# Self-attention of a two-layer decoder: four heads stored side by side at each key

## The chip, the core and the metric

The kernel runs on one NeuronCore of a Trainium2 chip. It computes in five engines: TensorE (PE; its weight loads are shown on a line of their own, PEld), VectorE (DVE), ScalarE (ACT), GpSimd (POOL) and SyncE (SP), which here only issues DMAs. The metric is the time of one execution on the device in microseconds (us), as a median over runs. All data is 32-bit floating point unless said otherwise, so one element is 4 bytes.

## The reference, cut to what matters

Eight batches of 256 tokens with 256 features go through two layers. Layer 0 is a gated recurrence, a cross-attention and a small feed-forward with quantised weights. Layer 1 is a self-attention with relative positions, a cross-attention and a gated feed-forward. Each step ends in a residual sum and a layer norm. The change touches layer 1's self-attention, with 16 heads of 16 features:

```python
idx = jnp.clip(pos[None, :] - pos[:, None], -MAX_REL, MAX_REL) + MAX_REL   # MAX_REL = 20
rk2, rv2 = rel_k[idx], rel_v[idx]
attn1 = jnp.einsum('bhqd,bhkd->bhqk', q, k)
attn2 = jnp.einsum('bhqd,qkd->bhqk', q, rk2)
attn = jax.nn.softmax((attn1 + attn2) / scale, axis=-1)
w1 = jnp.einsum('bhqk,bhkd->bhqd', attn, v)
w2 = jnp.einsum('bhqk,qkd->bhqd', attn, rv2)
```

Only 41 distances count: outside the band of 20 keys to either side of the query, all distances look alike.

## The kernel before, in words

**The order of the work.** Nothing is left to a scheduler at run time. While the program is built, the class `Order` (L87) plays the whole kernel through with costs that are written beside each step, and writes out the instructions of each engine in the order that this gives. A step asks for an engine, a cost in us, the times at which its inputs are ready, and buffers (`Slots`, `Held`). A DMA is given bytes and a rate in GB/s (`dma`, L208); the planner lets transfers follow one another on one memory clock (`memory`, L191). Each engine then runs its list in that order on the chip and waits where an input is late.

**Three attentions with one body.** The items of layer 0's cross-attention (`item_x0`, ai = 0), layer 1's self-attention (`item_s1`, ai = 1) and layer 1's cross-attention (`item_x1`, ai = 2), eight of each, share the functions `quad`, `head`, `values`, `scales` and `attend_out`. A quad is four heads, `head_of(n, j)` for j from 0 to 3, all even or all odd heads of one half c of the features. For each quad:

- PE computes scores into four PSUM banks, one per head, 2 x 256 wide (L914).
- DVE adds a bias to the scores, and finds the row minimum of the negated sum (L942; 256 keys an instruction). In cross-attention the bias is a mask tile; in self-attention it is the band of the quad, `band[:, j]`.
- ACT takes the exponential into `p[:, j, q, :]` and sums the row (L958; 256 keys an instruction).
- PE transposes `p[:, j]` in four pieces of 128 x 128 (L503, where `p` is the operand that is loaded as weights), and ACT or DVE copies the PSUM bank to a `pts` buffer (L291, L292). There are eight `pts` buffers. The buffer is asked for after the transposition (L976).
- PE multiplies by the values (L998).

In all three attentions `p` is [128, 4 heads, 2, 256 keys]: the 256 keys of one head lie next to one another.

**What self-attention does besides.** `to_scratch` (L1306) multiplies the queries with the 41 distances for all eight heads of a half (`drel`, L1317), copies the product to `w`, [128, 8 heads, 104], has POOL spread the last distance over the rest of each row (L1327), and writes it to a scratch array in HBM, `sk`. `to_bands` (L1346) reads `sk` back along diagonals, so that a distance becomes a key: four DMAs for each quad, which write the band tiles, [128, 4 heads, 2, 256 keys]. After the exponentials, `tails_task` (L1386) writes the part of `p` that lies in the band to a second scratch array, `pb` (L1399), and sums the rest: POOL cuts it out of `p` (L1410, L1415), DVE reduces it (L1426). The diagonals of `pb` come back as sums for each distance into `acc`, [128, 2, 2, 8 heads, 41] (L1434), `acc` is transposed (L1468) and multiplied with the relative values (L1483). The sums of the exponentials are kept in `acc` too, and `scales` takes their reciprocal (L1022).

Every one of these DMAs moves runs as long as the innermost stretch that is contiguous on both sides: 104 keys or fewer of one head for `sk`, `band` and `pb` (416 or 336 bytes), 39 distances of one head for `acc` (156 bytes).

**What overlaps.** The self-attention items and the cross-attention items of layer 1 are interleaved by `S1_AT` and `X1_AT` (L785). Band tiles are used from 309 to 653 us of the span.

Of the kernel before, what the change touches and what calls it, by code (L numbers as in the profile page):

```python
# [86 lines left out]
class Order:  # L87
# [51 lines left out]
    def run(self):  # L139
        while self.tasks:  # L140
# [3 lines left out]
            for task in sorted(self.tasks, key=lambda t: (t[0] >= FILLER, t[0], t[1])):  # L144
# [3 lines left out]
                if needs:  # L148
                    slots = needs[0].slots
                    if id(slots) in kept:  # L150
                        continue
                    if len(slots.idle) < len(needs):
                        if ready <= self.clock + 0.5:
                            kept.add(id(slots))
                        continue
                    slots.idle.sort()
                    ready = max(ready, slots.idle[len(needs) - 1][0])
# [17 lines left out]
            if best is None:  # L175
                ahead = [t[3][3] for t in self.tasks if t[3][0] == "get" and t[3][3] > self.clock + 0.5]
                if not ahead:
                    raise RuntimeError(f"stuck: {[t[3][:2] for t in self.tasks]}")
                self.clock = min(ahead)
                continue  # L180
            for held in task[3][4]:
                held.take(*held.slots.idle.pop(0))
# [40 lines left out]
def kernel(  # L223
# [119 lines left out]
    drel = const.tile([P, HH, NR], F32, name="drel")  # L343
# [5 lines left out]
    zero = w0.tile([P, LPAD], F32, name="zero")  # L349
    nc.gpsimd.memset(zero, 0.0)  # L350
    sk, pb = {}, {}
    for pr in range(2):
        for t in range(NQ):
            for c in range(KC):
                sk[pr, t, c] = scratch.tile(
                    [HH, P, SKW], F32, tag=f"sk{pr}{t}{c}", name=f"sk{pr}{t}{c}"
                )
        pb[pr] = scratch.tile([KC, NQ, HH, P, PBW], F32, tag=f"pb{pr}", name=f"pb{pr}")
# [71 lines left out]
    def loads_rel():  # L430
# [9 lines left out]
        for (pr, q, c), d in sk.items():  # L440
# [3 lines left out]
                    out=d[:, :, 0:LPAD].rearrange("h p w -> p h w"),  # L444
                    in_=zero.unsqueeze(1).to_broadcast([P, HH, LPAD]),
                ),
                90,
            )
        for d in pb.values():
            for c in range(KC):  # L450
                for q, (z0, p0) in enumerate(((0, 0), (PBW - MR, P - BLK))):
# [3 lines left out]
                            out=d[c, q, :, p0 : p0 + BLK, z0 : z0 + MR].rearrange("h p w -> p h w"),  # L455
                            in_=zero[p0 : p0 + BLK, 0:MR].unsqueeze(1).to_broadcast([BLK, HH, MR]),
# [3 lines left out]
        def tables():  # L460
            nc.vector.tensor_tensor(
                drel, blocks, blocks[:, :, 0:1].to_broadcast([P, HH, NR]), ALU.subtract
            )
# [8 lines left out]
        events["rel"] = yield from do("DVE", 0.8, [t], tables)  # L472
# [325 lines left out]

    def project_q(it, srcT, t_src):
# [153 lines left out]
    def head(it, n, j, p, s, nm, t, left, times):  # L953
        h = head_of(n, j)

        def emit():
            for q in range(NQ):
                nc.scalar.activation(  # L958
                    p.tile[:, j, q, :], s.tile[:, q, :], AF.Exp, bias=nm[:, q : q + 1], scale=-1.0,
# [12 lines left out]
        t = yield from do("PE", TURNS, [t_e, ps], lambda: transposed(ps.tile, p.tile[:, j]))  # L972
# [3 lines left out]
        pts = yield from get(pts_bufs, f"pts{it.name}_{n}_{j}", t)  # L976
# [41 lines left out]
    def scales(it):  # L1018
# [3 lines left out]
        t = yield from do("DVE", 0.3, [t_s], lambda: nc.vector.reciprocal(  # L1022
            rs.rearrange("p t (c h) -> p t c h", c=KC), it.sums_all()
        ))
# [102 lines left out]
    def item_x0(b):  # L1127
        it = Item(0, b, b, "l0a", "l0x")
        it.sum_of = lambda t, h: it.sums[:, t, h : h + 1]
        it.sums_all = lambda: it.sums.rearrange("p t (c h) -> p t c h", c=KC)  # L1130
# [135 lines left out]
    def layer1_self():  # L1266
        rel = layer1s.enter_context(tc.tile_pool(name="rel", bufs=1))
        kr_bufs = slots(rel, "kr", 2, [P, KC, 2, S - BW])
        wide_bufs = slots(rel, "wide", 2, [P, HH, PBW])
        acc_bufs = slots(rel, "acc", 2, [P, KC, NQ, HH, NA])  # L1270
# [4 lines left out]
        for n in range(3):  # L1275
            bands.append(rel.tile([P, 4, NQ, S], F32, name=f"band{n}"))
# [8 lines left out]
    def cleared(bands):  # L1285
        def emit():
            flat = t.rearrange("p j t k -> p (j t k)").rearrange("p (n k) -> p n k", k=P)
# [7 lines left out]
    def item_s1(b, kr_bufs, wide_bufs, acc_bufs, tail_bufs, at_bufs, band_bufs):  # L1295
# [7 lines left out]
        it.sum_of = lambda t, h: it.acc.tile[:, h // HH, t, h % HH, 0:1]  # L1303
        it.sums_all = lambda: it.acc.tile[:, :, :, :, 0].rearrange("p c t h -> p t c h")

        def to_scratch(c, t_sk):  # L1306
            q = it.q.tile
            out = []
            ends = it.ends[c] = small.tile([P, NQ, HH], F32, tag="ends", name=f"ends{b}_{c}")
            t_e = 0.0  # L1310
            for t in range(NQ):
# [6 lines left out]
                        flat(), q[:, c, t * P : (t + 1) * P], drel.rearrange("p h r -> p (h r)"),  # L1318
# [3 lines left out]
                rows_ = flat().rearrange("p (h r) -> p h r", r=NR)  # L1322
                t_w = yield from copy([t_p, w.at], w.tile[:, :, 0:NR], rows_, HH * NR)
                ps.drop(t_w)

                def emit():
                    nc.gpsimd.tensor_copy(  # L1327
                        w.tile[:, :, NR:], w.tile[:, :, NR - 1 : NR].to_broadcast([P, HH, PBW - NR])
                    )
                    nc.gpsimd.tensor_copy(ends[:, t, :], w.tile[:, :, NR - 1])  # L1330
# [6 lines left out]
                        out=sk[b % 2, t, c][:, :, LPAD:].rearrange("h p w -> p h w"), in_=w.tile  # L1337
                    ),
                    180,
# [6 lines left out]
        def to_bands(c, times, sk_set):  # L1346
            for i in range(2):
# [4 lines left out]
                def emit():  # L1352
                    for t, lo, hi in ((0, BLK + MR, BW), (1, P + BLK + MR, S)):
                        nc.gpsimd.tensor_copy(  # L1354
                            band.tile[0:BLK, :, t, lo:hi],
                            it.ends[c][0:BLK, t, i:HH:2].unsqueeze(2).to_broadcast([BLK, 4, hi - lo]),
# [4 lines left out]
                for t in range(NQ):  # L1361
                    for g in range(P // BLK):
# [4 lines left out]
                                out=band.tile[g * BLK : (g + 1) * BLK, :, t, lo:hi],  # L1367
                                in_=diagonals(
                                    sk[b % 2, t, c], 4, 2 * P * SKW, SKW - 1,
                                    i * P * SKW + g * BLK * SKW + LPAD + lo - k0, hi - lo,  # L1370
                                ),
                            ),
                            180,
# [12 lines left out]
        def tails_task(n, p, left, t_p):  # L1386

            c = n // 2
            own = slice(n % 2, HH, 2)
# [475 lines left out]
```

## Time and profile before

| what | before |
|---|---|
| median of 3 runs | 821.1 us (819.34 to 821.84) |
| profiled execution: span from first to last instruction | 807.4 us |
| what lies around the span, against the median | 13.7 us |
| mean granted TensorE clock | 0.998 |
| busy PE / DVE / ACT / POOL | 774.9 / 703.4 / 629.7 / 210.4 us |
| DMA packets on SP's queue | 177574, of which all but some 22500 are under 512 bytes |
| share of the 16 DMA engines' time that these packets take | 43.4% |

The profiled execution is given by its span alone; its own time is not listed apart from the three runs, so that what lies around the span is taken as 821.1 - 807.4 = 13.7 us, and a change of the span as a change of the time.

A group of instructions is shown as: line, engine, operation, written tile <- read tiles, shapes, count, then busy us and mean ns of one, then the idle time of the engine just before them with what ended it. Consecutive instructions of an engine overlap, so that a pace (start to start) is read from the timeline and not from the mean of one.

### The profile page before, as it was taken

The page shows a single profiled execution, that of the slowest core. Times are in us where ns is not written, and L with a number is a line of the kernel's source. Part 1 is how long each engine was busy: PE and PEld are TensorE (multiplying, and loading weights), DVE is VectorE, ACT ScalarE, POOL GpSimd, SP SyncE. Part 2 cuts the span into 40 slices and gives each one's busy share as a digit, 9 for nine tenths or more (in the row PEclk, how much of TensorE's full clock was granted, in tenths as well). Part 3 has the DMA queues.
Part 4 walks back from the last instruction along what each step waited for, and adds up shares of the span by engine and source line. Part 5 has one row for each costly group of instructions (what it writes and reads, how often), then busy time and mean ns, then how long its engine had stood idle before and what let it go on. Part 6 is the DMA issues. An engine that isn't in the chain of part 4 may idle for free. (4 is left out here: it accounts for less than half of the span.)

```text
span 807.4 us, 21273 instructions
## 1 busy us (share of the span) xinstructions
PE 774.9 (96%) x7175; PEld 597.3 (74%) x7175; DVE 703.4 (87%) x2461; ACT 629.7 (78%) x2036; POOL 210.4 (26%) x398
## 2 busy tenths in 40 slices
PE   7999999999999999997999999999999999999995
PEld 6787777777766787665767677767776767899885
DVE  3998989989787698887799999898898999989986
ACT  2339999899988457786597799999999899845942
POOL 4440321122111044233333304313242323110010
PEclk9999999999999999999999999999999999999999
DMA  5736352100100449889978706743656333100001
GB/s 183 221 120 97 26 74 50 40 15 28 40 14 15 144 116 220 173 166 154 192 159 170 137 7 145 166 87 89 121 120 139 85 72 114 40 15 16 26 14 39
DMA packets 177681, 77.67 MB, mean 96 GB/s; under 512 B 155046, under 2 KB 171430, under 8 KB 177574
## 3 DMA queue, kind: packets, MB, share of 16 engines
q1 hardware_dynamic: 177574, 76.32, 43.4%
q8 instruction: 57, 0.93, 0.5%
q14 instruction: 50, 0.41, 0.2%
HBM read 41.66 MB, written 34.64 MB: 94 GB/s over the span
## 5 line engine op out<-in xcount | busy, mean ns | idle before, releaser
L958 ACT ACTIVATE p<-sn,nm 128x256 f32<-128x256 f32 x768 | 381.5, 510 | 14.1 <-DVE nm L942 8.2
L503 PE MATMUL pt<-ident,p 128*128 128x128 f32 x1536 | 208.4, 278 | 4.3 <-ACT p L958 1.8
L503 PEld LDWEIGHTS pt<-ident,p 128*128 128x128 f32 x1536 | 169.4, 141 | 50.5 <-ACT p L958 30.2
L292 ACT COPY pts<-pt 128x512 f32<-128x512 f32 x277 | 148.3, 591 | 34.5 <-PE pt L503 29.6
L958 ACT ACTIVATION_READ_ACCUMULATOR p<-sn,nm 128x1 f32 x768 | 154.4, 201 | 0.0
L914 PE MATMUL s<-k,q 32*128 32x256 f32 (+2 forms) x1792 | 118.6, 370 | 0.5 <-ACT pts L292 0.3
L998 PE MATMUL pv<-pts,v 128*32 128x256 f32 x1536 | 104.0, 385 | 0.0
L942 DVE CUSTOM_DVE_ANT_0 sn<-s,bias 128x256 f32<-128x256 f32 x256 | 93.1, 419 | 10.0 <-ACT p L958 5.8
L942 DVE CUSTOM_DVE_ANT_0 sn<-s,hide 128x256 f32<-128x256 f32 x256 | 92.8, 418 | 8.2 <-PE s L914 5.3
L942 DVE CUSTOM_DVE_ANT_0 sn<-s,band 128x256 f32<-128x256 f32 x256 | 92.3, 418 | 8.6 <-PE s L914 3.5
L914 PEld LDWEIGHTS s<-k,q 32*128 32x128 f32 x1792 | 77.2, 185 | 30.1 <-issue 20.1
L291 DVE COPY pts<-pt 128x512 f32<-128x512 f32 x107 | 71.1, 683 | 6.7 <-PE pt L503 6.3
L998 PEld LDWEIGHTS pv<-pts,v 128*32 128x32 f32 x1536 | 41.7, 109 | 41.5 <-issue 19.1
L942 DVE DVE_READ_ACCUMULATOR2_ANT nm<- 128x1 f32 x768 | 63.0, 82 | 0.0
L1028 POOL COPY rsw<-rsum 128x512 f32<-128x512 f32 x24 | 14.6, 610 | 157.4 <-DVE rsum L1022 139.0
L520 PE MATMUL pso<-wvo,oT 128*128 128x256 f32 x192 | 46.3, 385 | 0.4 <-ACT pts L292 0.4
L520 PEld LDWEIGHTS pso<-wvo,oT 128*128 128x128 f32 x192 | 35.1, 190 | 7.8 <-issue 1.3
L1354 POOL COPY band<-ends 64x256 f32<-64x256 f32 x64 | 21.5, 360 | 70.8 <-DVE nm L942 70.8
L1426 DVE TENSOR_REDUCE acc<-tail 128x8 f32<-128x864 f32 x32 | 33.4, 1045 | 5.3 <-POOL tail L1415 5.3
L1327 POOL COPY w<-w 128x504 f32<-128x504 f32 x32 | 19.6, 613 | 68.8 <-DVE w L291 40.7
L1709 ACT ACTIVATE sg<-fg 128x512 f32<-128x512 f32 x24 | 14.3, 599 | 21.7 <-PE fg L1698 21.6
L520 PE MATMUL psv<-wvo,ctxT 128*128 128x256 f32 x128 | 30.8, 384 | 0.0
(197 smaller groups left out, 1321.3 us busy)
## 6 DMA issues: line engine op xcount, KB each, us to landing
sk<-w SPq DMA_DIRECT2D x32, 416.0 KB
band<-sk SPq DMA_DIRECT2D x64, 104.0 KB
pb<-p SPq DMA_DIRECT2D x64, 104.0 KB
band<-sk SPq DMA_DIRECT2D x64, 84.0 KB
pb<-p SPq DMA_DIRECT2D x64, 84.0 KB
acc<-pb SPq DMA_DIRECT2D x32, 156.0 KB
ctxT<-in_ctxT SPq DMA_DIRECT2D x16, 256.0 KB
wpad<-in_qk_w SPq DMA_DIRECT2D x6, 512.0 KB
```

Of the source, the lines that this page charges most:

```text
L291: ("DVE", on_dve(n), lambda: nc.vector.tensor_copy(dst, src)),
L292: ("ACT", on_act(n), lambda: nc.scalar.copy(dst, src)),
L503: nc.tensor.transpose(ps[:, c, t * P : (t + 1) * P], src[:, t, c * P : (c + 1) * P], ident)
L520: nc.tensor.matmul(ps[:, t, :], srcT[:, c, t * P : (t + 1) * P], w[:, c, :], start=(c == 0), stop=(c == KC - 1),)
L914: nc.tensor.matmul(ps[j].tile[:, t, first : first + w], it.q.tile[32 * j : 32 * j + 32, c, t * P : (t + 1) * P], k[32 * j : 32 * j + 32, c ...
L942: nc.vector.tensor_tensor_reduce(out=s.tile[:, t, :], in0=ps[j].tile[:, t, :], in1=tile[:, t, :], scale=-1.0, scalar=3e38, op0=ALU.add, op ...
L958: nc.scalar.activation(p.tile[:, j, q, :], s.tile[:, q, :], AF.Exp, bias=nm[:, q : q + 1], scale=-1.0, accum_out=it.sum_of(q, h),)
L998: nc.tensor.matmul(it.pv.tile[32 * j : 32 * j + 32, c, :], it.v.tile[:, k, head_of(n, j), :], pts.tile[:, k, :], start=(k == 0 and i == 0 ...
L1028: lambda: nc.gpsimd.tensor_copy(wide.tile.rearrange("p t (h d) -> p t h d", d=DH), rs.unsqueeze(3).to_broadcast([P, NQ, H, DH]),),
L1327: nc.gpsimd.tensor_copy(w.tile[:, :, NR:], w.tile[:, :, NR - 1 : NR].to_broadcast([P, HH, PBW - NR]))
L1354: nc.gpsimd.tensor_copy(band.tile[0:BLK, :, t, lo:hi], it.ends[c][0:BLK, t, i:HH:2].unsqueeze(2).to_broadcast([BLK, 4, hi - lo]),)
L1426: lambda: nc.vector.tensor_reduce(acc[:, c, :, own, 1], tail.tile, AX.X, ALU.add),
```

## The change

Wherever self-attention keeps four heads of a quad, the head becomes the innermost index. `drel` and `w` become [.., 2, 41 or 104, 4], `sk` and `pb` [.., row, key, 4], the bands [128, 2, 256 keys, 4], `acc` [.., 2, 41, 4]. Self-attention's `p` keeps its buffer but is read through `beside` and `probs` as [128, 2, 256 keys, 4]; the two cross-attentions use `p` as before. A run of a DMA is then four times as long (1664, 1344 or 624 bytes), the number of DMAs is the same, and an engine that works on one head of a band, of `p` or of `acc` finds its elements 16 bytes apart.

```diff
+    def beside(p):
+        return p.rearrange("p j t k -> p (j t k)").rearrange("p (t k j) -> p t k j", t=NQ, j=4)
+    def probs(it, p):
+        return p if it.whole else beside(p).rearrange("p t k j -> p j t k")
...
-                    p.tile[:, j, q, :], s.tile[:, q, :], AF.Exp, bias=nm[:, q : q + 1], scale=-1.0,
+                    probs(it, p.tile)[:, j, q, :], s.tile[:, q, :], AF.Exp, bias=nm[:, q : q + 1], scale=-1.0,
...
-        t = yield from do("PE", TURNS, [t_e, ps], lambda: transposed(ps.tile, p.tile[:, j]))
+        pts = Held(pts_bufs, f"pts{it.name}_{n}_{j}")
+        t = yield from do("PE", TURNS, [t_e, ps, pts], lambda: transposed(ps.tile, probs(it, p.tile)[:, j]))
...
-        pts = yield from get(pts_bufs, f"pts{it.name}_{n}_{j}", t)
...
-            bands.append(rel.tile([P, 4, NQ, S], F32, name=f"band{n}"))
+            bands.append(rel.tile([P, NQ, S, 4], F32, name=f"band{n}"))
...
-            quad(it, 0, parts, lambda n, j: (it.bands[n].tile[:, j], 0.0)),
+            quad(it, 0, parts, lambda n, j: (it.bands[n].tile[:, :, :, j], 0.0)),
...
-                                out=band.tile[g * BLK : (g + 1) * BLK, :, t, lo:hi],
+                                out=band.tile[g * BLK : (g + 1) * BLK, t, lo:hi, :].rearrange(
+                                    "p k j -> p (k j)"
+                                ),
...
-                            180,
+                            280,
...
-                            in_=p.tile[rows_, :, t, lo:hi],
+                            in_=beside(p.tile)[rows_, t, lo:hi, :].rearrange("p w j -> p (w j)"),
...
-                    tail.tile[:, 0], p.tile[:, :, 0, 0 : P - MR], [[0, 4], [-1, P - MR]], ALU.is_ge,
+                    tail.tile[:, 0], probs(it, p.tile)[:, :, 0, 0 : P - MR], [[0, 4], [-1, P - MR]], ALU.is_ge,
...
-                            it.acc.tile[:, c, t, 2 * j : 2 * j + 2, :].rearrange("p h r -> p (h r)"),
+                            it.acc.tile[:, c, t, :, :, j].rearrange("p i r -> p (i r)"),
```

Four smaller edits go with it. `scales` takes two reciprocals of [128, 2, 8], one for each half c, instead of one of [128, 2, 16], in all three attentions. The table `drel` is made by two subtractions instead of one. The rates that the planner gives these DMAs go up (zeroes for `sk` 90 to 200 GB/s, `sk`, `band` and `pb` 180 to 280, `acc` 125 to 220). And the planner changes: a step may ask for buffers of several kinds at once, a transposition (and a projection in `keys_values`) asks for its `pts` buffer together with its PSUM bank, before it and not after it, and where nothing can go on, a step of lower rank may take a buffer that one of higher rank is waiting for (`patient`):

```diff
-                if needs:
-                    slots = needs[0].slots
-                    if id(slots) in kept:
-                        continue
-                    if len(slots.idle) < len(needs):
-                        if ready <= self.clock + 0.5:
+                short = False
+                for slots in {id(x.slots): x.slots for x in needs}.values():
+                    count = sum(x.slots is slots for x in needs)
+                    if id(slots) in kept or len(slots.idle) < count:
+                        short = True
+                        if patient and ready <= self.clock + 0.5:
                             kept.add(id(slots))
                         continue
                     slots.idle.sort()
-                    ready = max(ready, slots.idle[len(needs) - 1][0])
+                    ready = max(ready, slots.idle[count - 1][0])
+                if short:
+                    continue
...
+                if not ahead and patient:
+                    patient = False
+                    continue
```

## The prediction

> **What bounds the kernel now.** I read the span in slices first, then busy time by stage, then the groups of the stage, then the waits for DMAs, and last the timeline for paces. Band tiles live from 309 to 653 us, so 300 to 680 us is the stage that the change works on. Busy time by stage (length; then PE, PEld, DVE, ACT, POOL with counts; clock; DMA share; GB/s):
>
> ```profile
> core 0: us, PE busy (x) PEld busy (x) DVE busy (x) ACT busy (x) POOL busy (x), PEclk, DMA share, GB/s
> 300.00:400.00 100.00, 92.29 (x880) 66.39 (x879) 83.63 (x276) 69.86 (x230) 36.78 (x88) 1.00 0.95 182
> 400.00:680.00 280.00, 276.72 (x2952) 203.58 (x2952) 257.50 (x988) 260.60 (x895) 83.67 (x165) 1.00 0.55 115
> 300.00:680.00 380.00, 369.01 (x3831) 269.96 (x3829) 341.12 (x1263) 330.45 (x1124) 120.45 (x252) 1.00 0.66 133
> ```
>
> Two things are to be seen. From 400 us on PE is busy for 98.8%, DVE for 92%, ACT for 93%: three engines are nearly full, PE sets the end, and none has room for a large addition. From 300 to 400 us the DMA engines are at 0.95 and PE is idle for 7.7 us: only there do transfers hold anything up, and even there mostly by the order that the planner wrote around them. Direct waits for a DMA are small: in the list of waits PE's longest one in that window is
>
> ```profile
> PE psa L1468 <- DMA acc<-pb: 1.7, 2, 1.4
> ```
>
> (us in total, times, longest), and DVE waits 0.9 us for bands in the whole span. So **transfers are not the bound; PE is, with DVE and ACT close behind.**
>
> The groups that the change touches, and the pace of transpositions in the timeline (start, length, count; chain of waits: start, length):
>
> ```profile
> L942 DVE CUSTOM_DVE_ANT_0 sn<-s,band 128x256 f32<-128x256 f32 x256 | 92.3, 418 | 8.6 <-PE s L914 3.5 <-ACT p L958 2.8 <-DMA band<-sk 0.9
> L958 ACT ACTIVATE p<-sn,nm 128x256 f32<-128x256 f32 x768 | 381.5, 510 | 14.1 <-DVE nm L942 8.2 <-POOL bias L1153 4.2 <-POOL tail L1410 1.4
> L503 PEld LDWEIGHTS pt<-ident,p 128*128 128x128 f32 x1536 | 169.4, 141 | 50.5 <-ACT p L958 30.2 <-issue 7.0 <-ACT pts L292 4.2
> L1468 PEld LDWEIGHTS psa<-ident,acc 128*82 128x82 f32 x128 | 13.0, 120 | 7.1 <-issue 4.0 <-DVE nm L942 0.9 <-PE pt L503 0.5
> ```
>
> ```profile
> 402.78 1.45 PEld L503 LDWEIGHTS pt<-ident,p 128*128 128x128 f32 x12
> ```
>
> ```profile
> 702.24 2.62 PE pt L503 x24
> ```
>
> ```profile
> 702.24 2.62 PE pt L503 x24
> ```
>
> 24 transpositions take 2.62 us, 109 ns each, and their weight loads come at (1.45 - 0.14)/11 = 119 ns: loads and multiplications run at one pace, so a slower load of `p` is a slower PE.
>
> **What goes.** The packets. 128 x 8 = 1024 pieces of each of the 32 writes of `sk`, 256 of each of 128 band reads and 128 writes of `pb`, 1024 of each of 32 reads of `acc`, 131,072 together, become a quarter; the zeroes (12,288) too. 107,520 of 177,574 packets go, about 70,000 stay. The trace's packet records give 31.8 ns for 416 bytes, 27.4 for 336, 17.9 for 156, 52.9 for 1024 and 99.4 for 2048; straight lines between these give about 82, 67 and 38 ns for the new sizes. In 16-engine time: before (65536 x 31.8 + 32768 x 27.4 + 32768 x 17.9) / 16 = 223 us, after (16384 x 82 + 8192 x 67 + 8192 x 38) / 16 = 138 us. The stage's share falls from 0.66 to about (251 - 85)/380 = 0.44. What it is worth is PE's idle time in the first 100 us, down to the later rate of 1.2%: 7.7 - 1.2 = **-6.5 us**. At the least it is worth 0; at the most all 11.0 us of PE's idle time in the stage, and some 10 more if a better plan also thins out PE's busy but stretched work.
>
> **What comes: elements 16 bytes apart.** Four kinds of instruction work on one head where its neighbours now lie between its elements: 256 of L942 (`band`, read), 256 of L958 (`p`, written), 512 loads at L503 and 128 at L1468 (`p` and `acc`, read), 64 of L1410 and L1415 (`p`, read). No bulk row of this trace has such a pitch, so each is bounded:
>
> - Lower end: nothing. An engine that takes an element a step anyway may not care. Below nothing there is no reason to look: no element less is moved.
> - Upper end: each element costs a second step. DVE: 512 elements take 683 ns (L291), 256 take 418, so 256 steps are 265 ns, x 256 = 68 us. ACT: 2048 elements take 1902 ns (L1288), 512 take 591, 0.85 ns a step, 218 ns x 256 = 56 us. PE: a pace of 109 ns is 128 steps, x 512 = 56 us; L1468 has 82 columns, 70 ns x 128 = 9 us; 65 us together. POOL: 570 ns more, x 64 = 36 us, against 260 us of idle time in the stage: hidden, unless POOL comes late for the reduction at L1426, which has waited 5.3 us for it so far.
>
> Two rows have single elements at a wide pitch. DVE's reciprocal reads `acc` 164 bytes apart and takes as long as from contiguous sums:
>
> ```profile
> L1022 DVE RECIPROCAL rsum<-sums x16: 319/348/355, 79.8 to 767.4; 128x32 f32<-128x32 f32 x16
> L1022 DVE RECIPROCAL rsum<-acc x8: 338/345/351, 351.9 to 658.7; 128x32 f32<-128x32 f32 x8
> ```
>
> [...] POOL's copy of `ends` reads 8 elements 416 bytes apart:
>
> ```profile
> L1330 POOL COPY ends<-w 128x8 f32<-128x8 f32 x32 | 6.9, 216 | 0.0
> L546 POOL TENSOR_SCALAR rs_l0x<-mv_l0x 128x2 f32<-128x2 f32 x8 | 1.5, 191 | 0.5
> L1327 POOL COPY w<-w 128x504 f32<-128x504 f32 x32 | 19.6, 613 | 68.8 <-DVE w L291 40.7 <-ACT w L292 28.0
> ```
>
> Six elements more than the two of L546 cost 25 ns, 4 ns each, where the contiguous copy costs (613 - 191)/502 = 0.84. The operations differ and the difference is small, but it is the nearest row, and it leans to the upper end. I take the upper end for reads and writes alike, and keep 0 for the range.
>
> With it: PE 369.0 + 65 = 434 us busy in the stage; at its present share of 97.1% that is 447 us for 380, **+67**. DVE 341 + 68 = 409: 421 at PE's share, 455 at its own of 89.8% (+41 to +75). ACT 330 + 56 = 386 (+18 to +64). The three additions lie on different engines and beside one another, so they don't add up; PE's sets the sum, since PE is what is full now. If only DVE pays, it is +41 before the relief, and if only ACT does, about +18.
>
> [...]
>
> **Edits with small prices.** [...] `drel` in two subtractions: once, ahead of the stage, 0. L1327, L1354, the copies to `w` and the tables' product keep their element counts with runs of four or more: 0. SP issues as many DMAs as before (614 ns each for bands): 0. Claiming `pts` ahead of the transposition adds no wait on the chip, since PE writes no `pts`; it only alters the written order, as the new rates do. Eight buffers against eight banks: ACT's copies of `pt` now idle 34.5 us before they start and PE's loads 4.2 us for those copies, so between -4 and +8 us; I take 0.
>
> **Sum.** 67 - 6.5 = 60.5, the small edits at 0: **+60.5 us**. Span 807.4 + 60.5 = 867.9; with the 13.7 us around it, 881.6, say 882, against the median of 821.1.
>
> **The rivals.** (1) *The pitch costs nothing and the transfers' relief is all there is*: faster, 821.1 - 6.5 = 814.6, in its own range 800 to 819. For it: DVE's two equal reciprocal rows. Against: POOL's row. It decides as soon as the second step is under about 10% of the upper end on PE, DVE and ACT, for then 6.5 is more than 0.1 x 67. (2) *Only some engines pay, or less than a step*: DVE alone 41 - 6.5 = +35, 856; ACT alone +12, 833; half a step everywhere 33 - 6.5 = +27, 848. Between 825 and 857. (3) *It does not do what it says in time*: the pitch is free and the order that the planner wrote hides transfers anyway, as DVE's 0.9 us of waiting for bands suggests: 821 +- 2.5. (4) *The pitch is free and the new order is worse*: the PE list with `pts` claimed early starves ACT's copies; +3 to +10, 824 to 831.
>
> **How the numbers follow.** The forecast (reads and writes pay about a step): 0.46, own range 858 to 907. Rival 2: 0.14. Rival 1: 0.31. Rival 3: 0.05. Rival 4: 0.04. This kernel's measurement can tell 0.3% (2.5 us) from no change. Faster: 0.31; same: 0.05; slower: 0.64. The range reaches from 806, which leaves out a fifth of rival 1, to 907: DVE's +75 without relief, the reciprocals' 2 and 8 of a worse order. By name that holds 0.9 of the chances; with what the bounds may miss, some 0.8.
>
> **What will show it.** L942's form with `band` apart from those with `bias` and `hide` (418 now; 680 by the forecast, 418 by rival 1). L958 the same: self-attention's exponentials 510 or 730. Loads at L503: 141 or some 250 for a third of them, and 24 in 2.6 us or in 5. POOL's cuts 570 or 1140. Packets about 70,000 in any case; if not, the change did not do what it says. The DMA share from 300 to 400 us should leave 0.95. I am wrong if L942's two forms stay equal and PE's loads keep 141 ns.

## The result, and the profile after

The changed kernel is slower: 853.3 us, median of four runs (852.69 to 855.28), against 820.5 us for the kernel before in the same comparison (819.34 to 821.84). The ratio is 1.0405, with a 95% interval of 1.0377 to 1.0433. The profiled execution has a span of 850.9 us and took 852.7 us, so only 1.8 us lie around the span. Against the 807.4 us of the kernel before, the span grew by 43.5 us.

In three later comparisons the kernel before took 812.1, 812.6 and 810.4 us, while the changed kernel, run again in the second of them, took 853.7. So a time is compared only with others of its own comparison, and ratios are used from one to the next. By the second of these the change costs 5.1%, 41 us. The changed kernel takes the same time in both; it is the kernel before that was slower in the first comparison, and why is not shown.

The packets first, by the row of SP's queue (packets, MB, share of 16 engines):

```profile
q1 hardware_dynamic: 70054, 76.32, 30.5%
```

The layout does what it says: 177,574 packets became 70,054 with the same bytes. Busy time by stage of the changed kernel, columns as in the prediction:

```profile
core 0: us, PE busy (x) PEld busy (x) DVE busy (x) ACT busy (x) POOL busy (x), PEclk, DMA share, GB/s
300.00:400.00 100.00, 91.84 (x905) 69.64 (x903) 97.28 (x281) 88.01 (x252) 41.43 (x73) 1.00 0.56 157
400.00:680.00 280.00, 261.65 (x2556) 192.96 (x2555) 254.14 (x852) 241.62 (x753) 92.44 (x157) 0.99 0.39 112
300.00:680.00 380.00, 353.49 (x3459) 262.60 (x3458) 351.42 (x1132) 329.63 (x1005) 133.87 (x229) 1.00 0.44 124
```

The DMA share of the stage fell from 0.66 to 0.44. But PE, which was busy for 98.8% from 400 us on, is now at 93.4% there, and from 300 to 400 us DVE is busy for 97.3% where it was for 83.6%. The first engine to be full in the stage is another one. The groups that the change touches:

```profile
L975 ACT ACTIVATE p<-sn,nm 128x256 f32<-128x256 f32 x768 | 418.1, 593 | 22.1 <-DVE nm L959 14.3 <-issue 6.2 <-POOL tail L1444 0.9
L512 PEld LDWEIGHTS pt<-ident,p 128*128 128x128 f32 x1536 | 182.3, 163 | 66.3 <-ACT p L975 33.2 <-issue 12.4 <-ACT pts L299 10.6
L959 DVE CUSTOM_DVE_ANT_0 sn<-s,band 128x256 f32<-128x256 f32 x256 | 143.6, 624 | 4.7 <-issue 2.1 <-PE s L931 1.3 <-DMA band<-sk 1.1
L959 DVE CUSTOM_DVE_ANT_0 sn<-s,bias 128x256 f32<-128x256 f32 x256 | 93.0, 419 | 11.2 <-PE s L931 7.6 <-ACT p L975 3.4
...
L1444 POOL TENSOR_SCALAR_AFFINE_SELECT tail<-p 128x432 f32<-128x432 f32 x32 | 32.0, 999 | 0.0
...
L1497 PEld LDWEIGHTS psa<-ident,acc 128*82 128x82 f32 x128 | 15.0, 157 | 5.9 <-issue 2.6 <-PE pt L512 1.0 <-ACT q L829 0.8
```

L959, L975, L512, L1444 and L1497 are L942, L958, L503, L1415 and L1468 of before. The two DVE rows are the same instruction on 256 elements; only the one that reads `band`, 16 bytes from element to element, went from 418 to 624 ns. Its busy time is 143.6 - 92.3 = 51.3 us more. A third of the exponentials are pitched, which puts the mean of all at 593 ns instead of 510. Who waits for whom in the stage (us in total, times, longest; PE alone, 300 to 680 us):

```profile
PE pt L512 <- DVE nm L959: 9.7, 16, 1.2
PE pt L512 <- ACT p L975: 2.9, 11, 0.6
PE s L931 <- DVE nm L959: 2.5, 5, 0.6
```

In the kernel before, PE's waits in this window for `nm`, the row minimum that DVE finds with the scores, were 1.5 us in all; the largest was

```profile
PE psq L509 <- DVE nm L942: 1.1, 1, 1.1
```

Now it is 9.7 + 2.5 us in two lines alone: PE stands behind DVE. ACT's pace is to be read from its timeline:

```profile
422.36 0.76 ACT L975 ACTIVATE p<-sn,nm 128x256 f32<-128x256 f32 x1
422.91 0.21 ACT L975 ACTIVATION_READ_ACCUMULATOR p<-sn,nm 128x1 f32 x1
422.97 0.76 ACT L975 ACTIVATE p<-sn,nm 128x256 f32<-128x256 f32 x1
```

A self-attention exponential takes 0.76 us, and one starts every 0.61 us. In the kernel before they took 0.50 and started every 0.49:

```profile
405.13 0.50 ACT L958 ACTIVATE p<-sn,nm 128x256 f32<-128x256 f32 x1
405.62 0.50 ACT L958 ACTIVATE p<-sn,nm 128x256 f32<-128x256 f32 x1
```

### The profile page after: what moved, and what is told of

Read it like the earlier page. It is cut to its first block, busy times and chain, and to the rows that moved or that the text cites. A ratio compares the mean times of both kernels' runs of the same rounds, so it can differ in the third digit from the quotient of the medians.

```text
span 850.9 us, 21229 instructions
## 1 busy us (share of the span) xinstructions
PE 800.2 (94%) x7175; PEld 617.7 (73%) x7175; DVE 752.2 (88%) x2480; ACT 667.5 (78%) x2044; POOL 237.6 (28%) x396
## 2 busy tenths in 40 slices
DMA packets 70161, 77.67 MB, mean 91 GB/s; under 512 B 12710, under 2 KB 63910, under 8 KB 70054
## 3 DMA queue, kind: packets, MB, share of 16 engines
q1 hardware_dynamic: 70054, 76.32, 30.5%
## 5 line engine op out<-in xcount | busy, mean ns | idle before, releaser
L975 ACT ACTIVATE p<-sn,nm 128x256 f32<-128x256 f32 x768 | 418.1, 593 | 22.1 <-DVE nm L959 14.3
L512 PE MATMUL pt<-ident,p 128*128 128x128 f32 x1536 | 221.6, 285 | 16.7 <-DVE nm L959 9.7
L512 PEld LDWEIGHTS pt<-ident,p 128*128 128x128 f32 x1536 | 182.3, 163 | 66.3 <-ACT p L975 33.2
L299 ACT COPY pts<-pt 128x512 f32<-128x512 f32 x266 | 143.6, 587 | 29.5 <-PE pt L512 28.3
L975 ACT ACTIVATION_READ_ACCUMULATOR p<-sn,nm 128x1 f32 x768 | 157.5, 205 | 0.0
L959 DVE CUSTOM_DVE_ANT_0 sn<-s,band 128x256 f32<-128x256 f32 x256 | 143.6, 624 | 4.7 <-issue 2.1
L931 PE MATMUL s<-k,q 32*128 32x256 f32 (+2 forms) x1792 | 125.1, 371 | 5.2 <-DVE nm L959 3.0
L931 PEld LDWEIGHTS s<-k,q 32*128 32x128 f32 x1792 | 82.4, 184 | 35.2 <-issue 15.8
L959 DVE CUSTOM_DVE_ANT_0 sn<-s,bias 128x256 f32<-128x256 f32 x256 | 93.0, 419 | 11.2 <-PE s L931 7.6
L959 DVE CUSTOM_DVE_ANT_0 sn<-s,hide 128x256 f32<-128x256 f32 x256 | 92.5, 419 | 9.3 <-PE s L931 5.8
L298 DVE COPY pts<-pt 128x512 f32<-128x512 f32 x118 | 78.8, 687 | 5.7 <-PE pt L512 4.9
L1015 PEld LDWEIGHTS pv<-pts,v 128*32 128x32 f32 x1536 | 42.5, 109 | 43.5 <-issue 18.1
L959 DVE DVE_READ_ACCUMULATOR2_ANT nm<- 128x1 f32 x768 | 65.7, 86 | 0.0
L1050 POOL COPY rsw<-rsum 128x512 f32<-128x512 f32 x24 | 14.7, 612 | 151.8 <-DVE rsum L1042 151.8
L1439 POOL TENSOR_SCALAR_AFFINE_SELECT tail<-p 128x432 f32<-128x432 f32 x32 | 31.5, 984 | 42.9 <-ACT p L975 23.0
L1455 DVE TENSOR_REDUCE acc<-tail 128x8 f32<-128x864 f32 x32 | 33.5, 1046 | 5.4 <-POOL tail L1444 5.3
L1444 POOL TENSOR_SCALAR_AFFINE_SELECT tail<-p 128x432 f32<-128x432 f32 x32 | 32.0, 999 | 0.0
```

Source lines behind the costliest of these rows:

```text
L298: ("DVE", on_dve(n), lambda: nc.vector.tensor_copy(dst, src)),
L299: ("ACT", on_act(n), lambda: nc.scalar.copy(dst, src)),
L512: nc.tensor.transpose(ps[:, c, t * P : (t + 1) * P], src[:, t, c * P : (c + 1) * P], ident)
L931: nc.tensor.matmul(ps[j].tile[:, t, first : first + w], it.q.tile[32 * j : 32 * j + 32, c, t * P : (t + 1) * P], k[32 * j : 32 * j + 32, c ...
L959: nc.vector.tensor_tensor_reduce(out=s.tile[:, t, :], in0=ps[j].tile[:, t, :], in1=tile[:, t, :], scale=-1.0, scalar=3e38, op0=ALU.add, op ...
L975: nc.scalar.activation(probs(it, p.tile)[:, j, q, :], s.tile[:, q, :], AF.Exp, bias=nm[:, q : q + 1], scale=-1.0, accum_out=it.sum_of(q, h),)
```

## The experiments

The question after the result was which of the slower steps sets the loss. The first runs still put the prediction's own step, that PE does, against DVE; the later ones put DVE's pitched read alone against PE's loads, ACT's pitched write, the order that the planner wrote, and a sum of several. Seven kernels take the pitch from one engine or several, or put it alone into the kernel before; the others run the changed kernel again, or try the order, the planner's prices and a narrower pitch. "Pitched" means 16 bytes from element to element.

**No engine pitched.** The layout of the transfers, the planner and the order stay; every engine reads and writes runs of 256.

```diff
-                    probs(it, p.tile)[:, j, q, :], s.tile[:, q, :], AF.Exp, bias=nm[:, q : q + 1], scale=-1.0,
+                    p.tile[:, j, q, :], s.tile[:, q, :], AF.Exp, bias=nm[:, q : q + 1], scale=-1.0,
...
-        t = yield from do("PE", TURNS, [t_e, ps, pts], lambda: transposed(ps.tile, probs(it, p.tile)[:, j]))
+        t = yield from do("PE", TURNS, [t_e, ps, pts], lambda: transposed(ps.tile, p.tile[:, j]))
...
-            quad(it, 0, parts, lambda n, j: (it.bands[n].tile[:, :, :, j], 0.0)),
+            quad(it, 0, parts, lambda n, j: (it.bands[n].tile.rearrange("p t k j -> p (t k j)").rearrange("p (j t k) -> p j t k", j=4, t=NQ)[:, j], 0.0)),
...
```

> The changed kernel with its transfers, order and buffers, but every engine takes the elements of the bands, of p and of acc in the order in which they lie (4 bytes apart), so that biases, probabilities and sums go to other heads and keys than in the reference: only the pitch is gone. Theory (the 16-byte pitch costs DVE, ACT, PE and POOL time for each element, and nothing else in the change costs anything): L959 with band back to 418 ns, self-attention's exponentials to 510, loads at L512 to 141, POOL's cuts to 570, time 806 to 822 us. Rival (the new written order is worse): the rows go back all the same, but the time stays at 840 to 853. Rival (several things, half each): 825 to 840.

814.0 us against 812.1, ratio 1.0016 (0.9990 to 1.0043): no difference. The rows of the stage and of the band read:

```profile
300.00:400.00 100.00, 96.25 (x1014) 72.41 (x1017) 84.25 (x297) 80.23 (x266) 38.96 (x87) 1.00 0.63 187
400.00:680.00 280.00, 271.98 (x2816) 198.81 (x2809) 253.83 (x970) 250.24 (x857) 78.30 (x154) 1.00 0.39 114
```

```profile
L959 DVE CUSTOM_DVE_ANT_0 sn<-s,band 128x256 f32<-128x256 f32 x256 | 92.3, 418 | 6.4 <-PE s L931 3.1 <-issue 2.0 <-ACT p L975 0.7
```

The band read is back at 418 ns, DVE at 84% in the first 100 us. So the loss comes with the pitch as a whole. And with the pitch gone, fewer packets and the new order together gain nothing over the kernel before.

**The old layout under the new planner.** The changed kernel's planner, rates and small costs on the layout of before, with its short runs.

```diff
-    drel = const.tile([P, 2, NR, 4], F32, name="drel")
+    drel = const.tile([P, HH, NR], F32, name="drel")
-                    [2, P, SKW, 4], F32, tag=f"sk{pr}{t}{c}", name=f"sk{pr}{t}{c}"
+                    [HH, P, SKW], F32, tag=f"sk{pr}{t}{c}", name=f"sk{pr}{t}{c}"
...
```

> The kernel before with the changed planner, the new rates and the new costs of the small steps, so that the instructions are written out in the order of the changed kernel, over the old layout with its short runs. Theory (pitch): 814 to 828 us, near the kernel before, since the order is neutral. Rival (order): 840 to 855. If the transfers matter at this order, whose rates promise more than the short runs give, waits for bands and acc grow from some 3 us to over 10 and the time lies between.

836.7 us, 1.0305 (1.0273 to 1.0337). This lies between the two ranges, as was expected if the transfers matter. The planner trusts transfers at the new rates, and they are late: POOL's L1334 waits 12.3 us once for a band read, PE 8.2 us for `acc`, DVE 7.3 us for bands. From here to the kernel with no pitch it is 836.7 - 814.0 = 22.7 us: that is what the long runs bring under the new order, and it makes good what that order costs with short ones. The granted clock is 0.985 to 0.986 in these runs and 0.991 to 0.996 in those with no pitch; if all time went with the clock, an estimated 7 us of the 22.7 would be the clock's.

**DVE alone contiguous.** Of the changed kernel only the band read is undone.

```diff
-            quad(it, 0, parts, lambda n, j: (it.bands[n].tile[:, :, :, j], 0.0)),
+            quad(it, 0, parts, lambda n, j: (it.bands[n].tile.rearrange("p t k j -> p (t k j)").rearrange("p (j t k) -> p j t k", j=4, t=NQ)[:, j], 0.0)),
```

> The changed kernel, but DVE reads the band contiguously (the biases of other heads and keys than in the reference); exponentials, transposes and cuts keep the pitch. Theory as in the prediction (PE is what is full and sets the sum): 206 ns x 256 = 53 us of DVE go, but the time falls by under 15 us, to 838 to 853. Rival (DVE has become the bound): 820 to 832.

827.4 us, 1.0191 (1.0159 to 1.0222). With ACT, PE and POOL still pitched (598 ns, 163 ns, some 1000 ns in their rows), 26 us of the loss of 41 are gone (1.0511 to 1.0191). The prediction's step, by which the time stays over 838, fails here; the rival's 820 to 832 holds. In the stage DVE is no longer the fullest engine:

```profile
300.00:680.00 380.00, 365.42 (x3677) 273.30 (x3676) 328.96 (x1208) 344.39 (x1068) 140.92 (x237) 1.00 0.44 127
```

**PE alone contiguous.** The exponential writes a permuted row at the same pitch, so that a load finds 128 neighbours; `acc` is loaded in runs too.

```diff
+                    (p.tile[:, j, q, :] if it.whole else p.tile[:, j, q, :].rearrange("p (x a) -> p a x", a=4)), (s.tile[:, q, :] if it.whole else s.tile[:, q, :].rearrange("p (a x) -> p a x", a=4)), AF.Exp, bias=nm[:, q : q + 1], scale=-1.0,
...
+        t = yield from do("PE", TURNS, [t_e, ps, pts], lambda: transposed(ps.tile, p.tile[:, j]))
...
```

> The changed kernel, but PE loads p and acc contiguously, while ACT still writes with a pitch of 16 bytes, inside each head's own 256 elements (keys in another order than in the reference), and DVE and POOL keep their pitch. Theory as in the prediction (PE sets the sum): loads at L512 back to 141 ns, some 40 ns a piece x 512 + 35 x 128 = 25 us go from PE, time 828 to 838 us. Rival (DVE or ACT sets it): 843 to 853. If DVE, ACT and PE each hold a part: 838 to 843.

851.7 us, 1.0495 (1.0460 to 1.0530). The loads are back at 140 and 120 ns, and the time does not answer: it lies in the range of the rival that DVE or ACT sets it, and DVE is busy for 95.94 us of the first 100.

**The changed kernel again,** unaltered, beside the next three.

> The changed kernel once more, on the chip of the runs beside it, as their reference: 1.040 of the kernel before, within 0.005.

853.7 us, 1.0511 (1.0476 to 1.0546). The expected ratio missed, because the kernel before took 812.6 here; the changed kernel's own time is the same within 0.5 us.

**ACT alone contiguous.** The exponential writes runs, and PE loads from these with the pitch that it had.

```diff
+        own = src.rearrange("p t k -> p (t k)").rearrange("p (x a) -> p a x", a=4)
+        for c in range(2):
+            for t in range(2):
+                nc.tensor.transpose(ps[:, c, t * P : (t + 1) * P], own[:, 2 * t + c, :], ident)
...
+                    p.tile[:, j, q, :], s.tile[:, q, :], AF.Exp, bias=nm[:, q : q + 1], scale=-1.0,
...
```

> The changed kernel, but ACT writes the probabilities contiguously, while PE loads them with a pitch of 16 bytes inside each head's own 512 elements (keys in another order than in the reference); DVE and POOL keep their pitch. Pairs of exponential and sum come every 0.61 us in the changed kernel and every 0.49 us before, so 0.12 x 256 = 31 us of ACT go. Theory now (DVE is full from 300 us on, and sets the time alone): 1.030 to 1.042 of the kernel before. Rival (DVE and ACT hold half of it each): 1.015 to 1.030.

854.0 us, 1.0522 (1.0487 to 1.0558): no gain. Both ranges started from a loss of 4.0%; against the changed kernel's 1.0511 in the same comparison, nothing came back, although 25 us of ACT's busy time leave the stage (329.63 to 304.35):

```profile
300.00:400.00 100.00, 91.35 (x903) 69.11 (x900) 97.24 (x279) 77.89 (x252) 41.35 (x72) 1.00 0.55 157
400.00:680.00 280.00, 259.80 (x2553) 191.69 (x2552) 254.79 (x851) 226.46 (x753) 91.92 (x157) 1.00 0.38 111
300.00:680.00 380.00, 351.15 (x3455) 260.80 (x3452) 352.02 (x1130) 304.35 (x1005) 133.28 (x228) 1.00 0.43 123
```

DVE's column is the changed kernel's to within 0.7 us in each row. ACT, made faster beside a full DVE, only idles more.

**The planner told the measured prices.** Four costs are altered, for DVE, ACT, PE and POOL (two are shown), and nothing else.

```diff
-            t = yield from do("DVE", 0.7, [t_s, t_b, t_bias, s.at], emit)
+            t = yield from do("DVE", 0.7 if it.whole else 1.1, [t_s, t_b, t_bias, s.at], emit)
-        t_e = yield from do("ACT", 1.0, [t, p.at], emit)
+        t_e = yield from do("ACT", 1.0 if it.whole else 1.24, [t, p.at], emit)
...
```

> The changed kernel, with the planner told the prices that the trace shows for self-attention: 1.1 us instead of 0.7 for a head's scores on DVE, 1.24 instead of 1.0 for its exponentials on ACT, 0.6 instead of 0.43 for its four transposes, 1.95 instead of 1.06 for POOL's cuts. Theory (the work on DVE is what costs): the copies that either engine may do go to ACT, and other work fills what is left; DVE still has 53 us more, so 1.020 to 1.035 of the kernel before. Rival (the loss lies in an order that was written with wrong prices): 1.000 to 1.015. Neither: 1.040.

839.1 us, 1.0352 (1.0305 to 1.0399), 14.7 us less than the changed kernel in the same comparison. DVE is busy for 359.6 us of the stage's 380 instead of 351.4:

```profile
300.00:680.00 380.00, 360.82 (x3579) 266.71 (x3578) 359.56 (x1160) 345.80 (x1051) 142.98 (x238) 1.00 0.46 133
```

About a third of the loss goes when the order is written with the measured prices. Which of the four prices matters was not separated.

**Two heads side by side instead of four.** The whole computation at a pitch of 8 bytes; runs are half as long, and by the prediction's count, not a measured one, SP's queue moves 177,574 - 143,360/2 = 105,894 packets.

```diff
...
-        return p.rearrange("p j t k -> p (j t k)").rearrange("p (t k j) -> p t k j", t=NQ, j=4)
+        return p.rearrange("p j t k -> p (j t k)").rearrange("p (m t k a) -> p m t k a", m=2, t=NQ, a=2)
...
```

> The changed kernel with two heads side by side and not four, computing the same as the reference: a pitch of 8 bytes, runs of 832, 672 and 312 bytes; two reductions and four cuts of half the size for one and two, which the planner isn't told; rates as in the changed kernel. Theory (what costs is that each element lies in a 16-byte stretch of its own): two elements share a stretch, and the rows go back to 418 (L973 or near it, band), 510 and 141 ns; time 0.998 to 1.015 of the kernel before. Rival (any pitch costs): 500 to 620, 560 to 750 and 160 to 230 ns, 1.02 to 1.045.

822.9 us, 1.0145 (1.0106 to 1.0183): the time is in the theory's range, at its upper end, and of the three rows two go back.

```profile
L960 DVE CUSTOM_DVE_ANT_0 sn<-s,band 128x256 f32<-128x256 f32 x256 | 92.6, 418 | 9.4 <-PE s L932 2.6 <-issue 2.1 <-POOL ends L1360 1.6
...
L513 PEld LDWEIGHTS pt<-ident,p 128*128 128x128 f32 x1536 | 180.4, 163 | 52.1 <-ACT p L976 30.1 <-issue 10.2 <-ACT pts L299 2.6
```

At 8 bytes DVE reads a band in 418 ns again, and the mean exponential is 517 ns, while PE's loads have the mean that they have at 16 bytes. What is left of the loss was not taken apart; PE's wait for `acc` (4.4 us), more POOL and DVE instructions of half the size (64 reductions of 591 ns for 32 of 1046) and PE's loads are the candidates.

**DVE's pitch alone, in the kernel before.** Its order, layout and transfers are untouched; one operand gets the pitch.

```diff
-            quad(it, 0, parts, lambda n, j: (it.bands[n].tile[:, j], 0.0)),
+            quad(it, 0, parts, lambda n, j: (it.bands[n].tile.rearrange("p j t k -> p (j t k)").rearrange("p (t k j) -> p t k j", t=NQ, j=4)[:, :, :, j], 0.0)),
```

> The kernel before, transfers, order and all, but DVE takes the band's elements 16 bytes apart from the same memory (biases of other heads and keys than in the reference). Theory (DVE's 53 us are the one price of the pitch that the time shows): 1.022 to 1.045 of the kernel before. Rival (PE is what is full, DVE has 39 us of idle time in the stage to take it up): 1.000 to 1.012.

849.6 us against 810.4, 1.0473 (1.0440 to 1.0505).

```profile
300.00:400.00 100.00, 88.72 (x781) 62.99 (x780) 91.02 (x252) 67.86 (x219) 33.98 (x80) 0.97 0.88 172
400.00:680.00 280.00, 263.72 (x2648) 190.45 (x2646) 261.65 (x882) 233.97 (x790) 78.63 (x160) 0.99 0.51 107
300.00:680.00 380.00, 352.44 (x3427) 253.44 (x3425) 352.67 (x1134) 301.83 (x1008) 112.61 (x240) 0.98 0.61 124
```

```profile
L942 DVE CUSTOM_DVE_ANT_0 sn<-s,band 128x256 f32<-128x256 f32 x256 | 143.0, 633 | 5.1 <-PE s L914 2.8 <-DMA band<-sk 1.4 <-issue 0.4
```

One operand of 256 instructions gives 39 us, nearly the whole loss and slightly more than the theory's range, and DVE's 352.7 us in the stage are close to the changed kernel's 351.4 while the DMA share is still 0.61. The other engines' instructions keep their means (510 ns for the exponentials, 142 for the loads, 567 for POOL's cuts). The granted clock is 0.986 to 0.990 in these four runs and 0.993 to 0.998 in those of the kernel before; if all time went with the clock, an estimated 7 of the 39 us would be the clock's. Whether DVE's pitch itself brings the clock down is not shown.

**PE's pitch alone, in the kernel before.** Only the loads of self-attention's `p` get it.

```diff
-        t = yield from do("PE", TURNS, [t_e, ps], lambda: transposed(ps.tile, p.tile[:, j]))
+        t = yield from do("PE", TURNS, [t_e, ps], lambda: transposed_own(ps.tile, p.tile[:, j]) if not it.whole else transposed(ps.tile, p.tile[:, j]))
```

> The kernel before, but PE loads the probabilities of self-attention 16 bytes apart, inside each head's own 512 elements (keys in another order than in the reference); acc is read as before. Loads 208 ns for 141, some 40 to 66 ns each in pace, x 512 = 20 to 34 us of PE. Theory now (PE's lists wait for DVE and ACT often enough to take it up): 1.000 to 1.012. The prediction's own step (PE is full, its additions set the sum): 1.020 to 1.040.

812.1 us against 810.4, 1.0015 (0.9997 to 1.0033): nothing. The two kinds of load:

```profile
L510 PEld LDWEIGHTS pt<-ident,p 128*128 128x128 f32 x1024 | 112.3, 140 | 32.6 <-ACT p L965 19.4 <-issue 5.2 <-ACT pts L292 2.7
...
L504 PEld LDWEIGHTS pt<-ident,p 128*128 128x128 f32 x512 | 68.5, 208 | 15.7 <-ACT p L965 9.8 <-issue 2.7 <-ACT pts L292 1.0
```

A load's duration goes from 140 to 208 ns, but the busy time for each goes only from 112.3/1024 = 110 to 68.5/512 = 134 ns, since loads overlap: 24 ns x 512 = 12 us. In the stage PEld's busy time grows by 9.3 us (269.96 to 279.24), that of the multiplications by 3.0 (369.01 to 372.02):

```profile
300.00:680.00 380.00, 372.02 (x3829) 279.24 (x3828) 339.30 (x1261) 330.82 (x1121) 119.86 (x252) 1.00 0.66 133
```

So most of a load's extra time never reaches PE's own line, and none of it lengthens the kernel in which PE was "busy for 98.8%".

**DVE and ACT contiguous,** PE and POOL pitched (the two edits of those experiments in one kernel).

> The changed kernel with DVE and ACT contiguous; PE loads the probabilities 16 bytes apart inside each head's own 512 elements (keys and heads in another order than in the reference), acc too, and POOL keeps its pitch. Of the 851.7 to 853.7 us of the changed kernel on two chips, DVE alone gave back 25, and all four engines 39. Theory (once DVE is contiguous ACT, busiest from 300 us on, is next): 812 to 820 us, nearly all of it. Rival (PE or POOL holds the other 13 us): 822 to 829.

820.5 us, 1.0116 (1.0083 to 1.0149), between the two ranges. Beside the kernel with DVE alone contiguous (1.0191), ACT's pitch is now worth 0.75%, some 6 us: it counts once DVE is out of the way. The last 1.0% down to 1.0016 lies between this kernel and the one with no pitch, which differ in PE's loads and POOL's cuts; these were not separated.

**The order alone, in the kernel before.** `pts` claimed ahead of the transposition, `patient`, and the claim in `keys_values`; layout, rates and costs of before.

```diff
+        pts = Held(pts_bufs, f"pts{it.name}_{n}_{j}")
-        t = yield from do("PE", TURNS, [t_e, ps], lambda: transposed(ps.tile, p.tile[:, j]))
+        t = yield from do("PE", TURNS, [t_e, ps, pts], lambda: transposed(ps.tile, p.tile[:, j]))
...
```

> The kernel before with the changed planner alone: buffers for transposes claimed ahead of them, and lower ranks let in where nothing can go on; old rates, old layout. The old layout in the changed kernel's order took 1.030 of the kernel before, with waits for late bands and sums. Theory (that order was written with rates that short runs don't reach): with rates that fit, 0.997 to 1.010. Rival (claiming the buffers early is what makes the order worse): 1.020 to 1.035.

827.0 us against 810.4, 1.0195 (1.0162 to 1.0228). I had expected no difference (up to 1.010); this is just under the rival's 1.020, so the order has a price of its own. The waits that grew:

```profile
POOL w L1334 <- DMA acc<-pb: 12.0, 1, 12.0
...
PE psa L1475 <- DMA acc<-pb: 8.3, 5, 4.7
```

PE's wait for `acc` was 1.7 us, and DVE falls from 83.6 to 74.5 us in the first 100 of the stage: by these rows the new order asks for what transfers bring sooner than short runs deliver it. The granted clock is 0.95 in these 100 us. Over the six runs it is 0.985 to 0.992, against 0.993 to 0.998 for the kernel before, so that up to some 6 of the 16.6 us could be the clock's by the estimate used above. The profiled execution took 830.9 us, 4 more than the median.

The runs that take the pitch from one engine or another, or add it to one, in one table:

| still pitched | ratio to the kernel before |
|---|---|
| none | 1.0016 |
| PE, POOL | 1.0116 |
| ACT, PE, POOL | 1.0191 |
| DVE, ACT, POOL | 1.0495 |
| DVE, PE, POOL | 1.0522 |
| all four (the change) | 1.0511 (1.0405 in the first comparison) |
| DVE alone, in the kernel before | 1.0473 |
| PE's loads of `p` alone, in the kernel before | 1.0015 |

## Why the prediction was right or wrong

The sign and the kind of loss were right: elements 16 bytes apart cost more than fewer packets bring. The time fell inside the range, but 29 us below the forecast of 882, in the place of the rival that only some engines pay or pay less than a step. That rival's price for DVE alone, 856, is close to the 853.3 measured, and this is in part luck: by spans it says +35 for a measured +43.5, and the 12 us too many that were added around the span hide most of the difference.

- **What bounds the kernel.** "PE is, with DVE and ACT close behind" did not stand up. Busy PE was not PE without room: 12 us more of loads disappeared in it, and its busy time in the stage grew by 3.0. That transfers do not bound it was not tested by itself; long runs and the new order together, with no pitch, have 40% of the packets and the time of before.
- **What goes.** The packets came out exactly (177,574 - 107,520 = 70,054). The stage's share, 0.44 and 0.44, agrees in part by luck: by the trace's records the new packets took 86.5, 82.0 and 40.3 ns for the 82, 67 and 38 of the forecast, so (16384 x 86.5 + 8192 x 82.0 + 8192 x 40.3) / 16 = 151 us for 138, while 380 us of the slower kernel hold less of the work (124 GB/s for 133). The -6.5 us is not seen: with no pitch, long runs and new order together bring nothing, and with short runs the new order costs. PE's idle time in the stage is 11.8 us in the kernel with no pitch, and was 11.0.
- **The failed step** is "PE's sets the sum, since PE is what is full now". DVE's sets it: 26 of 41 us go with its pitch alone, and 39 come with it alone, while PE's loads are worth nothing in either kernel. The step before it failed too: a load's extra time was added to PE's busy time in full, and of the 9.3 us that the pitched loads alone added to PEld in the stage, PE's line shows 3.0. The DVE term's +41 us at PE's share is near the +39 of the pitch on DVE alone, but by two errors that offset each other: 68 us of work where 51.3 were measured, at a share of 97.1% where DVE reached 92.5%. Worked out again with the measured 51.3 us, 341.1 + 51.3 = 392.4 us of DVE work at the share of the changed kernel, 351.42/380 = 0.925, need 424 us, 44 more than 380; the span grew by 43.5. That share is read off afterwards, so this shows that the sizes fit and forecasts nothing.
- **A second step for each element** was too much everywhere. DVE: 206 ns for 265, 51.3 us for 68. ACT: with two thirds of the 768 exponentials at 510 ns, (593 x 768 - 510 x 512)/256 = 759 ns, 249 longer for a forecast of 218, but in pace only 0.61 - 0.49 = 0.12 us, 31 us for 56, because the next exponential starts before the last one ends. PE: 68 ns in a load's duration, 24 in busy time, for 109; with `acc` (15.0 - 13.0) some 14 us for 65. POOL: some 420 ns for 570. PE was the term with the largest error, and the sum was hung on it.
- **The additions "don't add up".** Right: what ACT or PE pays beside a pitched DVE is worth nothing, by the two runs that take it from one of them. That POOL's cuts stay hidden there was not tested alone, but DVE's wait for them in the stage is 5.3 us as before.
- **The smaller edits at 0** was wrong by itself. Claiming `pts` early and `patient` cost 16.6 us with the short runs, over twice the bound of +8. It comes out near 0 only together with the long runs. I had looked for the price at the `pts` buffers alone; the waits that grew are for transfers. The reciprocals take 228 and 232 ns for each half against 345 for the whole; by busy time, in which overlaps count once, they take 6.2 + 3.0 = 9.2 us against 5.5 + 2.8 = 8.3: 0.9 us of DVE. The 2 us that the range of the prediction has for them are shown by no run; these 0.9 us are what the runs showed in their place.
- **What lies around the span.** I took 13.7 us; the changed kernel's listed runs have 1.8, and those of the kernel before in the later comparisons some 2. So the 821.1 us and the span of 807.4 can hardly be of executions of one speed, and the span grew by 43.5 us where the median in the first comparison grew by 32.8.

By pitch, DVE and ACT agree: a pitch of 16 bytes lengthens a band read and an exponential (418 to 624 ns, 510 to 759), and one of 8 does so little or not at all (418, and a mean of all exponentials of 517 for 510). PE's loads differ, since their mean is the same 163 ns at 8 as at 16, for 141 before. That each element has a 16-byte stretch of its own, the theory of the run with two heads, fits DVE and ACT and not PE's loads; these two pitches alone were run, and no mechanism is shown.

What stays open: how the last 1.0% divides between PE's loads and POOL; what the long runs would bring under the order of before, which was not run; what is left in the kernel with two heads side by side; why the kernel before took 820.5 us in the first comparison and 810 to 813 later; and what lowers the granted clock in the three kernels with short runs that lost time. No version that was run beats the kernel before. The kernel with two heads side by side is the fastest of those that compute the whole reference in a changed layout, and it is 1.06% to 1.83% slower.

## What to carry to other kernels

A layout that suits a DMA was paid for here by every engine that reads or writes it, and most of the price that showed was one engine's. Price each engine's extra work, take it from that engine alone in a run, and doubt the busy share of an engine whose instructions overlap: PE, at 97%, took up 12 us more of loads, and DVE, at 90%, could not take up 51. Idle time is not room either: DVE had 39 us of it in the stage, and of 51 us more 39 lengthened the kernel. Before a pitch of four words is taken, try two: here it left DVE as it was (418 ns) and ACT nearly so (a mean of 517 ns for 510). Where an order is written out beforehand, a change in its rules is an edit with a price of its own, and it has to be run alone; the costs that the order is written with belong to it, since the measured ones took back a third of the loss.

## What the runs showed of the hardware that was not expected

- DVE's instruction on 256 elements took 418 ns with those of one operand 8 bytes apart, as with contiguous ones; 16 bytes apart it took 624, 206 ns more, 0.8 ns an element.
- PE's weight load of 128 columns took 140 ns with contiguous elements and 208 with a pitch of 16 bytes. With one of 8 bytes the mean of all loads is the same 163 ns as with 16; the pitched third was not timed by itself there. Of the 68 ns at 16 bytes, 24 show in busy time and none in the kernel's time (1.0015).
- POOL's selection of 432 elements went from 570 to some 1000 ns at 16 bytes, 1 ns more an element.
- ACT's pitched write lengthened an exponential by 249 ns but the distance to the next by 120: in the timeline the next one starts 0.15 us before it ends (422.97 and 423.12), where before it was 0.01 (405.62 and 405.63).
